# Rings, load distance and MLP order at the end of a four-layer network kernel

## The chip, the cores and the metric

The kernel runs on one core of a Trainium2 chip. The metric is device time in microseconds; the kernel before has a median of 9638.22 us over three runs (9626.88 to 9641.67). Everything is float32.

## The reference

Four layers, each `x + layer(group_norm(x))`, on `x` of 8 x 384 x 32 x 32: (0) a Mamba block, (1) deformable convolutions, (2) a Mamba block with an MLP behind it, (3) a shift layer. The change is at the end of layer 2 and in layer 3.

```python
# layer 2, after the scan
t = y @ out_proj_w.T
t = gelu(t @ mlp_w1.T + mlp_b1) @ mlp_w2.T + mlp_b2        # 384 -> 1536 -> 384
# layer 3: 48 groups of 8 channels, each with its own offset
disp = _displace(x, round(offset))                          # zero outside the image
kernel = exp(-|grid + offset - round(offset)|^2 / 0.5)      # 5 x 5, normalized
out = depthwise_conv(disp, kernel)
```

The 5 x 5 kernel is a product of a column and a row factor, so displacement and convolution together are one 32 x 32 matrix over y and one over x for each group of channels.

## The kernel before, in words

One program does the four layers one after another. Layers 0 and 2 share `ssm_layer`. It goes over 16 steps (8 samples, two halves of TS = 512 tokens), and each step has 48 units (6 blocks of 128 channels, 8 pairs of states) of the scan. PE, ScalarE (ACT), VectorE (DVE) and GpSimd (POOL) get their instructions in an order written out by hand (`plan` and the loop after it). SP, which issues most DMAs, isn't in that list (`ENGINES`), so the framework's scheduler orders SP's queue; an engine's queue is worked off in order.

In layer 2 the output projection and the MLP of a step run beside the next step's scan. For the last step there is no next scan, and they stand after the loop, together with preparations of layer 3:

- `out_proj` (L500) for three blocks of output channels, `out_take` (L517, ACT) copies them to `t`.
- `kernels_a` (L1455 to L1481) and `kernels_b` (L1486 to L1500) make the matrices of the shift layer: small DVE and ACT work, at the end four ACT copies into `sbd` (L1500).
- The MLP goes over three quarters of its 1536 hidden channels, q = 0, 1, 2, each of four blocks of 128 (`NF // 4` is 3). `mlp_up` (L528) makes four products into PSUM (`ps_h`, from a ring of three buffers), `up_take` (L535, ACT) adds the bias and writes them to `hid` (one buffer, pool `p1`), `gelu` (L538, ACT) works on the whole `hid`, `mlp_down` (L545) makes three products from it (`ps_m`, the same PSUM ring), and `down_take` (L552, L554, DVE) adds them to `x`. At q = 2 it also stores the block to the DRAM tensor `x3s` (L506, SP).
- `stat_load` (L1506) and `stat` (L1512, L1514, DVE) gather the group norm's statistics of layer 3 from the 15 earlier half samples; `some(5)` does five of them in each q, and `stat(last, ...)` does the last half sample's as its blocks are finished.
- Weights come by `w_mid` (L246, SP) into the ring `wm` of three buffers.

The shift layer is `shift_parts`. It has 12 tiles m (`NM`) of 4 groups of 8 channels: 128 partitions are 4 groups x 32 rows, the free dimension is 8 channels x 8 samples x 32 columns. A half tile is a piece c (24 in all) of 128 x 1024. For each piece: `scale` (L1592, POOL) multiplies by the norm's factor; `over_y` (L1602, L1604, PE) applies the matrix over y and adds the norm's offset into the PSUM tile `ps_y`; `turn` (L1608, DVE) transposes 32 x 32 blocks into `syt`; `over_x` (L1614, PE) applies the matrix over x; `turn_back` (L1620, DVE) transposes back into `szt`; `add` (L1625, POOL) adds to the tile `sxr`. After the second piece 32 stores go out (L1629), 16 from SP and 16 from ACT's queue, each of 32 partitions and one channel to `out`, in runs of 32 floats. `load` (L1573) brings a tile by four DMAs from SP.

`main` is a software pipeline: in iteration i it emits `scale(i+3)`, `over_y(i+2)`, `over_x(i+1)`, `turn(i+2)`, `turn_back(i+1)`, `add(i)`. The first three tiles are loaded before it, and tile m is loaded three tiles ahead:

```python
for m in range(3):
    load(m)
norms()
main()
```

Buffers come from rings (a pool's tag with a number of buffers) left over from the scan: `bc` with 8 buffers of 8 KB per partition, `hs` with 4 and `db` with 3 of 4 KB, `wm` with 3 of 6 KB. Before, `sxr` and `sxa` (the scaled tile) both come from `bc`, as do the statistics' half samples `sx` and the tables `se`, `skr` and `ssel`; `syt` comes from `hs`, `szt` from `db`. `norms` (L1523 to L1563) finishes the statistics and makes the table `stab` that `scale` and `over_y` read.

Of the kernel before, what the change touches and what calls it, by code (L numbers as in the profile page):

```python
# [8 lines left out]
F32 = mybir.dt.float32  # L9
# [6 lines left out]
P = 128  # L16
C = 384
G = C // P
# [5 lines left out]
NS = 16  # L24
RK = C // 16
RB = RK + 2 * NS
TS = L // 2
W_MID = 1536
# [6 lines left out]
NF = FF // P  # L35
# [49 lines left out]
class Net:  # L85
# [107 lines left out]
    def ssm_layer(self, li, src, dst, shift=None):  # L193
# [3 lines left out]
        with ExitStack() as ctx:  # L197
            wp = ctx.enter_context(tc.tile_pool(name=f"w{li}", bufs=1))
            p1 = ctx.enter_context(tc.tile_pool(name=f"p1_{li}", bufs=1))
            p2 = ctx.enter_context(tc.tile_pool(name=f"p2_{li}", bufs=2))  # L200
# [32 lines left out]
            def v(i):  # L233
                return vec[:, i : i + 1]
# [8 lines left out]
            def w_mid(src, k):  # L243
                t = p2.tile([P, k, W_MID // k], F32, name="wm", tag="wm", bufs=3)
                n = src.shape[2]
                nc.sync.dma_start(out=t[:, :, :n], in_=src)  # L246
                return t
# [97 lines left out]
            def exp_ln():  # L345
                nc.scalar.preload_act_table_set("natural_log_exp_and_others")
# [155 lines left out]
            def store(s, o):  # L502
                if mlp:

                    y = s["h"] * H // 2
                    nc.sync.dma_start(  # L506
                        out=shift[0][o * P : (o + 1) * P, y : y + H // 2, s["b"] * W : (s["b"] + 1) * W],
                        in_=s["x"][:, o, :].rearrange("p (y x) -> p y x", x=W),
                    )
                if o == G - 1 and (not mlp or s is not steps[-1]):  # L510
                    nc.sync.dma_start(out=dst(s["b"])[:, :, s["sl"]], in_=s["x"])
# [11 lines left out]
            def mlp_up(s, q, f):  # L523
                if f == 0:
                    s["w1"] = w_mid(w1_d[:, :, q * 4 * P : (q + 1) * 4 * P], G)
                s["up", f] = ps = self.psum("ps_h")
                for k in range(G):
                    nc.tensor.matmul(  # L528
                        ps, s["w1"][:, k, f * P : (f + 1) * P], s["t"][:, k, :], start=(k == 0), stop=(k == G - 1)
                    )  # L530

            def up_take(s, q, f):
                if f == 0:
                    s["hid"] = p1.tile([P, 4, TS], F32, name="hid")
                nc.scalar.activation(s["hid"][:, f, :], s["up", f], AF.Identity, bias=v(V_B1 + 4 * q + f))  # L535

            def gelu(s):
                nc.scalar.activation(s["hid"], s["hid"], AF.Gelu)  # L538

            def mlp_down(s, q, o):  # L540
                if o == 0:
                    s["w2"] = w_mid(w2_d[:, 4 * q : 4 * q + 4, :], 4)
                s["down", o] = ps = self.psum("ps_m")
                for f in range(4):
                    nc.tensor.matmul(  # L545
                        ps, s["w2"][:, f, o * P : (o + 1) * P], s["hid"][:, f, :], start=(f == 0), stop=(f == 3)
                    )

            def down_take(s, q, o):
                xo = s["x"][:, o, :]  # L550
                if q == 0:
                    nc.vector.scalar_tensor_tensor(xo, s["down", o], v(V_B2 + o), xo, ALU.add, ALU.add)  # L552
                else:
                    nc.vector.tensor_tensor(xo, xo, s["down", o], ALU.add)  # L554
                if q == NF // 4 - 1:
                    store(s, o)

            steps = []
# [88 lines left out]
            with tc.manual_schedule(engines=ENGINES):  # L647
                s = steps[0]
# [29 lines left out]
                for i, (s, j, m) in enumerate(units):  # L678
                    c, t = divmod(i, T)
# [38 lines left out]
                    k = 3 if mine else 2 if m in gp_add else 1  # L718
# [16 lines left out]
                if mlp:  # L735
                    kernels_a()

                    def some(n):
                        for _ in range(min(n, len(stats))):
                            i = stats.pop(0)  # L740
                            for g in range(G):
                                stat(i, loaded["x", i], g)
                            if i + 6 < last:
                                stat_load(i + 6)

                    for q in range(NF // 4):
                        for f in range(4):
                            mlp_up(s, q, f)
                            up_take(s, q, f)
                        gelu(s)  # L750
                        if q == NF // 4 - 1:
                            exp_ln()
                        some(5)
                        if q == 0:
                            kernels_b()
                        for o in range(G):
                            mlp_down(s, q, o)
                            down_take(s, q, o)
                            if q == NF // 4 - 1:
                                stat(last, s["x"], o)  # L760
                    for m in range(3):
                        load(m)
                    norms()
                    main()
# [656 lines left out]
    def shift_parts(self, wp, p2, dap, src_of, srcs, dst):  # L1421
        nc, ins, nb = self.nc, self.ins, self.nb
        NM = NP // IG
        NQ = P // IG
        M2 = 2 * NM
        d = {}

        def ring(tag, shape, name, bufs=None):
            kw = {"bufs": bufs} if bufs else {}
            t = p2.tile(shape, F32, name=name, tag=tag, **kw)  # L1430
            return t

        def bc(name, *shape):
            t = ring("bc", [P, 2, 2, TS], name, NS // 2).rearrange("p a b l -> p (a b l)")
            n = 1
            for k in shape:
                n *= k
            return t[:, :n]
# [126 lines left out]

        NI = CPP * nb
        CH = NI * W // 2

        def load(m):
            xr = d["xr", m] = bc("sxr", NI, W).rearrange("p (i w) -> p i w", w=W)  # L1570
            for n in range(IG):
                c = (m * IG + n) * CPP
                nc.sync.dma_start(  # L1573
                    out=xr[n * H : (n + 1) * H].rearrange("p (k b) w -> p k (b w)", k=CPP),
                    in_=srcs[c : c + CPP].rearrange("k y b -> y k b"),
                )

        def table(c, t):
            m, h = divmod(c, 2)
            g, q = divmod(m, NQ // CPP)  # L1580
            q = q * CPP + h * CPP // 2
            return d["tab"][:, t, g, q : q + CPP // 2].rearrange("p q b -> p (q b)")

        def piece(t, c):
            return t[:, c % 2 * NI // 2 : (c % 2 + 1) * NI // 2].rearrange("p i w -> p (i w)")

        def scale(c):
            m = c // 2
            if c % 2 == 0:
                d["xa", m] = bc("sxa", NI, W).rearrange("p (i w) -> p i w", w=W)  # L1590
            x, xa = (piece(d[k, m], c).rearrange("p (i w) -> p i w", w=W) for k in ("xr", "xa"))
            nc.gpsimd.tensor_tensor(xa, x, table(c, 0).unsqueeze(2).to_broadcast([P, NI // 2, W]), ALU.mult)  # L1592

        def mat(c, t):
# [1 line left out]

        def over_y(c):
            ps = d["psy", c] = dap.tile([P, 2, TS], F32, name="ps_y", tag="da").rearrange("p a b -> p (a b)")[:, :CH]
            xa = piece(d["xa", c // 2], c)
            for i in range(0, CH, HL):  # L1600
                o = ps[:, i : i + HL]
                nc.tensor.matmul(o, mat(c, 1), xa[:, i : i + HL], start=True, stop=False)  # L1602
                t = table(c, 1)[:, i // W : i // W + HL // W].unsqueeze(2).to_broadcast([P, HL // W, W])
                nc.tensor.matmul(o.rearrange("p (i w) -> p i w", w=W), mat(c, 1), t, start=False, stop=True)  # L1604

        def turn(c):
            yt = d["yt", c] = ring("hs", [P, 2, TS], "syt", 4).rearrange("p a b -> p (a b)")
            nc.vector.transpose(yt, d["psy", c])  # L1608

        def over_x(c):  # L1610
            d["psx", c] = []
            for i in range(0, CH, HL):
                ps = self.psum("ps_yx")
# [1 line left out]
                d["psx", c].append(ps)  # L1615

        def turn_back(c):
            zt = d["zt", c] = ring("db", [P, 2, TS], "szt", 3).rearrange("p a b -> p (a b)")
            for i, ps in enumerate(d["psx", c]):
                nc.vector.transpose(zt[:, i * HL : (i + 1) * HL], ps)  # L1620

# [12 lines left out]
        def main():  # L1634
            nch = 2 * NM
            for i in range(-3, nch):
                for k, fn in ((3, scale), (2, over_y), (1, over_x), (2, turn), (1, turn_back), (0, add)):
                    if 0 <= i + k < nch:
                        fn(i + k)
                m = i // 2 + 3  # L1640
                if i % 2 and 3 <= m < NM:
                    load(m)

        return d, load_consts, kernels_a, kernels_b, stat_load, stat, norms, load, main
# [93 lines left out]
```

## Time and profile before

| | |
|---|---|
| median of three runs | 9638.22 us |
| profiled execution | 9640.38 us |
| its span, first to last instruction | 9638.6 us |
| mean granted TensorE clock | 0.948 |
| busy in the span: PE, DVE, ACT, POOL | 89%, 84%, 68%, 60% |
| last unit of the scan ends on PE | about 9329 us |
| last MLP and its output projection on PE | 9329.1 to 9419.9 us |
| last statistics on DVE | 9421.6 us |
| first `scale`, last `add` ends | 9432.5, 9629.4 us |

The profile is of one execution. A matmul line is named as line, operation, output and input; a wait line says which instruction waited for which other, with total us, number and longest. In a line of the timeline the brackets at the end give the engine's idle time before the instruction and what ended it. A "q" behind an engine's name means its DMA-issuing queue. Instructions that only issue a DMA don't count as busy. Ends of matmuls are modelled, so neighbouring groups can overlap by some tenths of a microsecond. From 9318 us on, PE is busy for 245 us of 321, POOL for 103, DVE for 117.

### The profile page before, as it was taken

The numbers are of one execution on the slowest core, as the hardware profiler recorded it, in microseconds if no ns is written. First come the engines' busy times: TensorE is split into PE (matmuls) and PEld (weight loads), VectorE is DVE, ScalarE is ACT, GpSimd is POOL, SyncE is SP. The second block draws the span as 40 slices with busy tenths as digits, with TensorE's granted clock in tenths as the row PEclk, the third lists the DMA queues.
The fourth block names the chain that finished last, engine by engine and source line by source line (L and its number), as shares of the span: only waits on it lengthen the run. The fifth ranks groups of instructions, "written<-read, shape, count | busy, mean of one in ns | idle before, by whom it ended". The sixth has DMA issues, their size and how long they took to land. (4 is left out here: it accounts for less than half of the span.)

```text
span 9638.6 us, 87976 instructions
## 1 busy us (share of the span) xinstructions
PE 8594.0 (89%) x28252; PEld 4554.4 (47%) x28252; DVE 8105.5 (84%) x8807; ACT 6508.4 (68%) x10236; POOL 5755.9 (60%) x3788
## 2 busy tenths in 40 slices
PE   6898888888886899999999997699999999999987
PEld 2333333333332677677677776234343443434333
DVE  6999999999996678778778777799999999999973
ACT  5666666666663677778778777667767777776750
POOL 6888888888895000000000000799999999999964
PEclk8999999999998999999999998799999999999998
DMA  2211211121121333333333333133332333223426
GB/s 71 83 58 46 83 52 52 54 81 52 49 80 45 74 77 83 87 81 83 87 82 83 87 81 85 59 121 99 93 93 89 117 111 96 90 91 101 125 95 108
DMA packets 560755, 792.02 MB, mean 82 GB/s; under 512 B 238019, under 2 KB 391011, under 8 KB 536601
## 3 DMA queue, kind: packets, MB, share of 16 engines
q1 hardware_dynamic: 508056, 779.99, 27.8%
q10 hardware_dynamic: 52224, 6.30, 0.4%
q8 instruction: 225, 3.69, 0.2%
q14 instruction: 250, 2.04, 0.1%
HBM read 716.49 MB, written 69.66 MB: 82 GB/s over the span
## 5 line engine op out<-in xcount | busy, mean ns | idle before, releaser
L426 POOL TENSOR_TENSOR db<-du,bc 128x1024 f32<-128x1024 f32 x1536 | 3608.4, 2354 | 421.0 <-DVE hs L436 229.1
L436 DVE TENSOR_TENSOR_SCAN da<-da,db 128x1024 f32<-128x1024 f32 x1272 | 2912.2, 2289 | 200.8 <-ACT da L421 151.0
L467 PE MATMUL y<-hs,ident 128*128 128x512 f32 x5184 | 2610.3, 639 | 384.8 <-DVE hs L450 242.1
L421 ACT ACTIVATE da<-dt,na 128x512 f32<-128x512 f32 x3072 | 2120.2, 691 | 912.9 <-DVE hs L450 683.4
L394 POOL TENSOR_TENSOR dt<-dt,sp_e 128x512 f32<-128x512 f32 x192 | 244.0, 1271 | 3091.0 <-DVE sp_e L386 3091.0
L467 PEld LDWEIGHTS y<-hs,ident 128*128 128x128 f32 x5184 | 1018.2, 203 | 1872.9 <-issue 1142.6
L1407 PE MATMUL wacc<-fsm,fxk 128*128 128x221 f32 (+34 forms) x10624 | 1636.4, 312 | 73.3 <-DVE fsm L1377 71.4
L450 DVE TENSOR_TENSOR hs<-da,bc 128x1024 f32<-128x1024 f32 x1272 | 1557.6, 1225 | 117.1 <-PE y L467 12.7
L1407 PEld LDWEIGHTS wacc<-fsm,fxk 128*128 128x128 f32 x10624 | 1550.0, 193 | 209.3 <-DVE fsm L1377 132.4
L1377 DVE TENSOR_TENSOR fsm<-fhy,fhx 128x170 f32<-128x170 f32 (+42 forms) x3216 | 1172.2, 427 | 430.5 <-PE wacc L1407 415.2
L1337 ACT ACTIVATE fhy<-fpyx,cell 128x416 f32<-128x416 f32 (+9 forms) x1280 | 645.6, 576 | 398.2 <-DVE fsm L1377 398.2
L1095 PE MATMUL ps_off<-fxn,fow 128*32 128x248 f32 (+18 forms) x2944 | 832.7, 523 | 3.8 <-issue 2.0
L1360 DVE TENSOR_TENSOR fxk<-fxt,fwk 128x1024 f32<-128x1024 f32 (+1 forms) x688 | 785.8, 1178 | 6.4 <-ACT fxt L1153 6.4
L436 DVE TENSOR_TENSOR_SCAN hs<-da,db 128x1024 f32<-128x1024 f32 x264 | 602.3, 2282 | 70.2 <-POOL db L414 28.0
L447 POOL TENSOR_TENSOR hs<-hs,bc 128x1024 f32<-128x1024 f32 x264 | 621.8, 2355 | 37.8 <-ACT st L442 37.5
L454 POOL TENSOR_TENSOR hs<-hs 128x512 f32<-128x512 f32 x480 | 609.0, 1269 | 3.5 <-DVE hs L450 3.5
L545 PE MATMUL ps_m<-hid,wm 128*128 128x512 f32 x1152 | 540.4, 614 | 39.7 <-ACT hid L538 34.8
L528 PE MATMUL ps_h<-t,wm 128*128 128x512 f32 x1152 | 536.0, 603 | 16.4 <-DVE x L552 16.4
L1342 ACT ACTIVATE fhy<-fhy,cols 128x1344 f32<-128x1344 f32 (+10 forms) x368 | 530.7, 1442 | 12.0
L1095 PEld LDWEIGHTS ps_off<-fxn,fow 128*98 128x98 f32 (+2 forms) x2944 | 352.7, 147 | 382.2 <-issue 359.2
L442 ACT COPY st<-da 128x2 f32<-128x2 f32 x624 | 97.8, 157 | 506.0 <-DVE hs L450 504.5
L545 PEld LDWEIGHTS ps_m<-hid,wm 128*128 128x128 f32 x1152 | 222.2, 196 | 343.6 <-issue 263.6
(192 smaller groups left out, 9626.7 us busy)
## 6 DMA issues: line engine op xcount, KB each, us to landing
bc<-bcd SPq DMA_DIRECT2D x256, 1024.0 KB
fpyx<-fposd SPq DMA_DIRECT2D x640, 256.0 KB
wm<-in_w SPq DMA_DIRECT2D x96, 768.0 KB
x<-x SPq DMA_DIRECT2D x71, 768.0 KB
winr<-in_win SPq DMA_DIRECT2D x192, 192.0 KB
x<-in_x SPq DMA_DIRECT2D x40, 768.0 KB
fpyx<-fposd SPq DMA_DIRECT2D x24, 1024.0 KB
wm<-in_wout SPq DMA_DIRECT2D x48, 384.0 KB
```

The costliest lines, as they stand in the source:

```text
L421: nc.scalar.activation(da[:, i, :], s["dt", j], AF.Exp, scale=na[:, j, n : n + 1])
L426: nc.gpsimd.tensor_tensor(db, du, s["bc"][m][:, 0], ALU.mult)
L436: nc.vector.tensor_tensor_scan(h1, da1, db1, 0.0, ALU.mult, ALU.add)
L447: nc.gpsimd.tensor_tensor(s["hs", m], s["hs", m], c, ALU.mult)
L450: nc.vector.tensor_tensor(hs, s["da", m], c, ALU.mult)
L467: nc.tensor.matmul(s["y"], self.ident, s["hs", m][:, i, :], start=first and i == 0, stop=k == NU - 1 and i == n - 1,)
L545: nc.tensor.matmul(ps, s["w2"][:, f, o * P : (o + 1) * P], s["hid"][:, f, :], start=(f == 0), stop=(f == 3))
L1095: nc.tensor.matmul(o[:, ya - r0 : yb - r0, xa:xb], ow[:, (dy + pad) * K + dx + pad, :], x3[:, ya + dy : yb + dy, xa + dx : xb + dx], start ...
L1337: nc.scalar.activation(hy[:, at : at + (yb - ya) * W], pyx[:, 0, ya * W : yb * W], AF.Abs, bias=bias)
L1360: nc.vector.tensor_tensor(t[:, :n], x, wk[:, j : j + 1, :].to_broadcast([P, n, P]), ALU.mult)
L1377: nc.vector.tensor_tensor(self.sub(sm, at, [(r * w, n), (w, r), (1, w)]), self.sub(hy, hy_at[by] + xa, [(r * W, n), (W, r), (1, w)]), self ...
L1407: nc.tensor.matmul(a[:, ya - 4 * o : yb - 4 * o, xa:xb], k, self.sub(sm, sm_at[by], [(w, yb - ya), (1, w)]), start=False, stop=False,)
```

## The change

The rings of layer 3 are given out anew: the scaled pieces `sxa`, now one buffer for each half tile, take `hs`; `syt` takes `db`; `szt` takes `wm`; the loaded tiles `sxr` keep `bc`. Six tiles are loaded before `main`, and each later tile six tiles ahead. In the last step's MLP the first products of a third come ahead of the second products of the third before it (up 0, up 1, down 0, up 2, down 1, down 2), so two `hid` are alive: the one of q = 1 of the last step takes a buffer of `bc`. The statistics are divided 4, 6 and 5 instead of 5, 5 and 5, and from q = 1 on they stand after `down_take` instead of before `mlp_down`.

```diff
             def up_take(s, q, f):
                 if f == 0:
-                    s["hid"] = p1.tile([P, 4, TS], F32, name="hid")
+                    if s is steps[-1] and q == 1:
+                        t = p2.tile([P, 2, 2, TS], F32, name="hid1", tag="bc", bufs=NS // 2)
+                        s["hid"] = t.rearrange("p a b l -> p (a b) l")
+                    else:
+                        s["hid"] = p1.tile([P, 4, TS], F32, name="hid")
+                    s["hid", q] = s["hid"]
...
-                        ps, s["w2"][:, f, o * P : (o + 1) * P], s["hid"][:, f, :], start=(f == 0), stop=(f == 3)
+                        ps, s["w2"][:, f, o * P : (o + 1) * P], s["hid", q][:, f, :], start=(f == 0), stop=(f == 3)
...
-                    for q in range(NF // 4):
-                        for f in range(4):
-                            mlp_up(s, q, f)
-                            up_take(s, q, f)
-                        gelu(s)
-                        if q == NF // 4 - 1:
-                            exp_ln()
-                        some(5)
+                    NQ = NF // 4
+                    for q in range(NQ + 1):
+                        if q < NQ:
+                            for f in range(4):
+                                mlp_up(s, q, f)
+                                up_take(s, q, f)
+                            gelu(s)
+                            if q == NQ - 1:
+                                exp_ln()
                         if q == 0:
+                            some(4)
                             kernels_b()
+                            continue
                         for o in range(G):
-                            mlp_down(s, q, o)
-                            down_take(s, q, o)
-                            if q == NF // 4 - 1:
+                            mlp_down(s, q - 1, o)
+                            down_take(s, q - 1, o)
+                            if q == NQ:
                                 stat(last, s["x"], o)
-                    for m in range(3):
+                        some(6)
+                    for m in range(6):
                         load(m)
...
+        AHEAD = 6
...
         def scale(c):
             m = c // 2
-            if c % 2 == 0:
-                d["xa", m] = bc("sxa", NI, W).rearrange("p (i w) -> p i w", w=W)
-            x, xa = (piece(d[k, m], c).rearrange("p (i w) -> p i w", w=W) for k in ("xr", "xa"))
+            d["xa", c] = ring("hs", [P, 2, TS], "sxa", 4).rearrange("p a b -> p (a b)")
+            x, xa = (t.rearrange("p (i w) -> p i w", w=W) for t in (piece(d["xr", m], c), d["xa", c]))
...
-            xa = piece(d["xa", c // 2], c)
+            xa = d["xa", c]
...
-            yt = d["yt", c] = ring("hs", [P, 2, TS], "syt", 4).rearrange("p a b -> p (a b)")
+            yt = d["yt", c] = ring("db", [P, 2, TS], "syt", 3).rearrange("p a b -> p (a b)")
...
-            zt = d["zt", c] = ring("db", [P, 2, TS], "szt", 3).rearrange("p a b -> p (a b)")
+            zt = ring("wm", [P, G, W_MID // G], "szt", 3).rearrange("p a b -> p (a b)")
+            zt = d["zt", c] = zt[:, :CH]
...
-                m = i // 2 + 3
-                if i % 2 and 3 <= m < NM:
+                m = i // 2 + AHEAD
+                if i % 2 and AHEAD <= m < NM:
                     load(m)
```

## The prediction, made before the result was known

> **What bounds the kernel now.** I read the page's engine slices first: only the last of 40 changes character (POOL's row ends 9, 9, 6, 4 and DMA's rises). The diff touches the end of layer 2 and the shift layer alone: its hid ring edit asks for the last step, and for every other step the new key of `hid` names the same tile. So I read the waits of 9318 to 9640 us, then the timelines of that stretch, then small windows of DMA. The columns of waits are total us, times, longest us.
>
> ```profile
> DVE syt L1608 <- PE ps_y L1604: 136.1, 24, 12.6
> POOL sxa L1592 <- DMA out<-sxr: 74.9, 8, 10.2
> POOL sxa L1592 <- DMA sxr<-x3s: 10.0, 1, 10.0
> PE ps_y L1602 <- POOL sxa L1592: 46.9, 9, 7.0
> PE ps_m L545 <- ACT hid L538: 9.4, 3, 4.0
> ```
>
> POOL's scaling of a new tile waits for DMA 9 times, 84.9 us, PE waits for POOL and DVE for PE: one chain, begun by DMA. SP's own waits:
>
> ```profile
> SPq L1629 <- POOL sxr L1625: 35.8, 13, 10.9
> SPq L1573 <- DMA out<-sxr: 30.9, 12, 4.1
> SPq L1629 <- DMA out<-sxr: 26.5, 28, 1.5
> ```
>
> SP waits for POOL too, so it is a circle. One turn of it, from SP's and POOL's timelines:
>
> ```profile
> 9513.83 12.86 SPq L1629 DMA_DIRECT2D out<-sxr  x16
> 9526.79 4.78 SPq L1573 DMA_DIRECT2D sxr<-x3s  x4
> ```
> ```profile
> 9518.64 1.91 POOL L1592 TENSOR_TENSOR sxa<-sxr,stab 128x1024 f32<-128x1024 f32 x1 [9.83 <-DMA out<-sxr]
> 9536.20 1.91 POOL L1592 TENSOR_TENSOR sxa<-sxr,stab 128x1024 f32<-128x1024 f32 x1 [9.17 <-DMA out<-sxr]
> ```
>
> The scaling at 9518.64 lets `add` run; it ends at 9522.9, the second half of that tile's stores is issued from 9522.9 to 9526.7, the loads of the tile three ahead stand behind them in SP (9526.8 to 9531.6), and when they have landed the scaling at 9536.20 starts. From 9482.10 to 9609.03, seven turns take 18.1 us each. Nothing is full in that time: 4.25 us of POOL a half tile (1.91 + 2.34), 2.5 us of DVE, and 5.15 us of PE (its L1614 groups start at 9441.72, 9446.87, 9452.02 and 9457.17 while input is there), so 10.3 us a tile.
>
> The last MLP before it, on PE:
>
> ```profile
> 9344.54 10.46 PE L528 MATMUL ps_h<-t,wm 128*128 128x512 f32 x24
> 9359.01 12.26 PE L545 MATMUL ps_m<-hid,wm 128*128 128x512 f32 x24 [4.00 <-ACT hid L538]
> 9371.11 10.46 PE L528 MATMUL ps_h<-t,wm 128*128 128x512 f32 x24
> 9384.29 10.57 PE L545 MATMUL ps_m<-hid,wm 128*128 128x512 f32 x24 [2.72 <-ACT hid L538]
> 9394.69 10.46 PE L528 MATMUL ps_h<-t,wm 128*128 128x512 f32 x24
> 9407.88 11.99 PE L545 MATMUL ps_m<-hid,wm 128*128 128x512 f32 x24 [2.72 <-ACT hid L538]
> ```
>
> Each second product waits for the gelu of its own first product: 9.44 us idle, and 1.8 and 1.5 us more where a group runs slow after it.
>
> **What the Trainium skill says.** "TensorE: Matmul & The Clock Gate", Part 1, What's actually happening: after an idle window of about 3.4 us the array runs at half its clock until it has been busy for about as long. The trace agrees: after 5 to 7 us of idle a pair of L1602 takes 2.07 us, and 1.02 in a full stretch. "DMA: Bandwidth & Descriptors", Why small descriptors are slow: there is a fixed cost per packet and per descriptor. The trace agrees: stores go out in 128 B runs and move 121 GB/s, loads in 1 KB runs 199. The columns after the stretch are busy us of PE, PEld, DVE, ACT and POOL with counts, then PE clock, DMA share and GB/s:
>
> ```profile
> 9514.50:9518.50 4.00, 0.41 (x1) 0.00 (x0) 1.18 (x2) 0.00 (x0) 0.00 (x0) 1.00 1.02 199
> ...
> 9628.00:9636.00 8.00, 0.00 (x0) 0.00 (x0) 0.00 (x0) 0.00 (x0) 1.37 (x1) 0.58 0.79 121
> ```
>
> The first row is loads with few stores, the second stores alone. The same page, Rules for kernel authors, says that DMAs of SP and ACT run on the same 16 engines and that spreading them saves only issue time; SP's and ACT's stores beside each other do not go over 121 GB/s here, so I add stores and loads up, not their queues.
>
> **The change part by part.** The profiled run took 9640.38 us and its span 9638.6, so 1.8 lie outside; its run stands 2.2 above the median 9638.22. I sum on the span and carry the difference to the median.
>
> MLP. Removed: the three gelu waits (9.44 us) and the slow starts (3.3), as PE now does up 0, up 1, down 0, up 2, down 1, down 2. Six groups of 10.45 from 9344.5 end at 9407.2, where they end at 9419.9 now. Cover: gelu 0 is done at 9358.95, up 1 runs to 9365.4. Added: `hid1` takes a buffer of the bc ring, so its first write can wait for one; `se` is free after L1495 (9350.2), `skr` after the sbd copies. Those four copies (0.92 each) stand ahead of up_take 1 on ACT and end at 9362.2; behind them PE's fourth group of up 1 needs a PSUM buffer (three in the ring) at 9362.8. I take 0; bounds 0 and 4 us (a whole sbd pass uncovered); no gain is possible from an added wait. w1 of q 1 is wanted 16 us earlier (9355, not 9371); SP issued it at 9344.5 with w2; 768 KB at the 199 GB/s of the loads above are 3.9 us, 7.9 if it shares, so it is in time; bound 0 to 4 us again. up 2 writes `hid` after down 0 has read it: PE's own order covers it.
>
> What comes last is then DVE, not PE. A statistics step costs 2.13 us (10.9 us for five, 9371.98 to 9382.86). `some(6)` stands after down_take 0 (9376.6) and costs 12.8, to 9389.4, as down 1 delivers: covered. The last five stand after down_take 1 (9397.5) and cost 10.2 (as 9395.5 to 9405.7), to 9407.7, and only then come three times 0.69 + 0.69 + 0.21, to 9412.7. Now it is 9421.57. So the MLP is worth **8.9 us**, not 12.7. `some(4)` and kernels_b after the first gelu lie in DVE time that waits for PE. norms and tables follow as now, so the first half tile's store starts at 9446.95 - 8.9 = 9438.1.
>
> Shift layer, six loads ahead. Three more tiles are 12 DMAs of 256 KB, and 24 in all stand in SP ahead of the first stores. They start when the last x3s write is issued (9411.7) and go every 1.3 us when the engines are full (9426.84, 9428.19, 9429.47 now), to 9443: 6 us of them are left at 9438.1. The first tile's four are first in line, so the first scaling isn't late. After that a load of tile m stands behind the stores of tile m - 6, and is used about four tiles of PE time later: at 10.3 us a tile that is 41 us, against 9 to 10 us that POOL waits now. So the 84.9 us of POOL's wait go.
>
> Rings. sxa leaves bc for hs (four half tiles, three ahead plus the one read), so bc's eight hold xr alone: seven tiles are alive between load and store, and one spare covers stores that land. syt moves to db (three; alive for two iterations), szt to wm (three, as it had). No instruction is added; waits for these rings: 0, bound 0 to 0.4 us a half tile (4 against 3 buffers of syt, one of PE's L1614), 0 to 10 us.
>
> What is late next: PE or DMA. **PE**: first product at 9434.85 - 8.9 = 9425.9, 24 half tiles at 5.15 are 123.6, so 9549.5; from PE's last end (9625.5) to the span's end are 13.1 us now: 9562.6. **DMA**: a tile is 1.05 MB, 8.7 us of stores at 121 GB/s and 5.2 us of loads at about 200. From 9438.1: 6 of loads left over, 12 x 8.7 = 104 of stores, 6 x 5.2 = 31 of loads: 141 us, so 9579.6, and 2.4 from the last issue (9636.2 now) to the end: **9582.0**. Stores used only 0.79 of DMA; if loads filled the rest (6.9 us a tile, 82 in all) it would be 9560 and PE would decide. Upward, mixed stretches stall SP; at 15 us for a tile with loads instead of 13.9 it is 9589. I take the sum without overlap, since 9527 to 9530, with both kinds, showed a share of 0.79 as well.
>
> Issue time is no bound: 0.5 us each, 16 + 4 a tile on SP is 10 us, and 16 on ACT is 8.
>
> Sum: 9582.0 - 9638.6 = -56.6, of which 8.9 are the MLP. Median 9638.2 - 56.6 = **9582**.
>
> **The rivals.** (1) Forecast, DMA paces: 9570 to 9605. (2) PE paces, loads slip into the stores' gaps: 9562.6 in span, 9562 median. For it: the share of 0.79; against: SP's 28 waits of stores on stores. (3) POOL's wait is exchanged for SP's own: stores keep 12.8 us and loads 4.8 a tile as in the timeline, now not as an echo of POOL. Six tiles at 17.6 and six at 12.8 are 182, so 9438.1 + 182 + 2.4 = 9623, median 9622. For it: 57.4 us of SP's waits are for DMA. Against: in the drain, 32 stores take 9.1 us. (4) Slower: each of a tile's four loads waits for a store of the tile whose buffer it takes, in SP, with the next tile's stores queued behind it. At the longest such wait, 4.1 us, that is 16.4 + 12.9 of stores, 29.3 us for the six tiles with loads: 6 x 29.3 + 6 x 12.9 = 253, so 9438 + 253 + 2.4 = 9693, median 9693. It makes the kernel slower from 20.2 us a tile on (six of them with six at 12.9 reach 9638.6). Against: the buffer is that of a tile stored a tile or two before.
>
> **How the numbers follow.** (1) 0.60, (2) 0.20, (3) 0.14, (4) 0.06. The predicted time is that of (1). About 0.2% (19 us) is what can be told from no change, so faster is below 9619. (1), (2) and a third of (3) are faster: 0.85; the rest of (3) is the same: 0.09; (4) slower: 0.06. The range takes (2) with 4 us below and (1) with the 4 us bounds of the MLP and the rings' 10: 9558 to 9613.
>
> **What would show it.** Right: no wait of sxa on DMA to speak of; PE's shift groups 5.15 us apart to about 9550; the last adds by 9555, and then a tail of stores alone of 15 to 25 us; DMA share near 0.8 from 9440; ps_m without a wait on hid; the last statistics at 9412 to 9413, behind other statistics on DVE. Wrong: PE gaps of 5 us or more between tiles (3 or 4), the tail shorter than 12 us (2), or a wait for w1 or hid1 at 9355 to 9363.

## The result and the profile after

| | before | after |
|---|---|---|
| median | 9637.44 us (4 runs) | 9606.45 us (4 runs, 9605.35 to 9607.43) |
| ratio, 95% interval | | 0.9969 [0.9952, 0.9987] |
| profiled execution, its span | 9640.38, 9638.6 us | 9605.35, 9603.5 us |
| MLP: start of the last `out_proj` to first `ps_y` | 105.8 us | 98.0 us |
| shift layer: first `ps_y` to the span's end | 203.7 us | 180.6 us |
| `scale` waits for a load | 9 times, 84.9 us | 3 times, 26.6 us |

The median fell by 31.0 us, and the two stretches give the same sum: 7.8 + 23.1 = 30.9. The prediction had 8.9 + 47.7 = 56.6; the 24.6 us that are missing from the shift layer (47.7 - 23.1) are the question. So the MLP did nearly what was forecast, and the shift layer half of it. Where `out_proj` starts differs by up to 12 us between profiles, with every layer ahead of it unchanged. So from here on stretches are compared, and medians, but not single spans.

The MLP on PE, from the timeline after:

```profile
9340.39 18.19 PE L528 MATMUL ps_h<-t,wm 128*128 128x512 f32 x42
9358.73 2.84 PE L528 MATMUL ps_h<-t,wm 128*128 128x512 f32 x6 [0.15 <-ACT hid L540]
9361.41 10.46 PE L550 MATMUL ps_m<-hid,wm 128*128 128x512 f32 x24
9371.71 10.46 PE L528 MATMUL ps_h<-t,wm 128*128 128x512 f32 x24
9382.01 20.76 PE L550 MATMUL ps_m<-hid,wm 128*128 128x512 f32 x48
```

Six groups follow each other without a gap but one of 0.15 us; the three waits for gelu (9.44 us) are gone.

The waits that answer to those of before (total us, times, longest us), first those of the engines, then those of SP's own queue:

```profile
DVE syt L1618 <- PE ps_y L1614: 89.7, 24, 13.4
...
POOL sxa L1602 <- DMA out<-sxr: 26.6, 3, 10.2
...
PE ps_y L1612 <- POOL sxa L1602: 14.8, 3, 8.1
```
```profile
SPq L1584 <- DMA out<-sxr: 32.0, 13, 6.7
...
SPq L1640 <- DMA out<-sxr: 22.0, 20, 5.4
SPq L1584 <- DMA sxr<-x3s: 17.7, 17, 2.3
...
SPq L1640 <- DMA sxr<-x3s: 8.3, 2, 6.2
```

Nine waits of POOL are three now, each about as long as before. SP's wait for POOL (35.8 us before) is down to 0.3 us, but its loads (L1584) wait for *stores* as long as before, 32.0 against 30.9 us, and the longest such wait has grown from 4.1 to 6.7 us. One turn of what is left, from SP's and POOL's timelines:

```profile
9511.00 8.57 SPq L1640 DMA_DIRECT2D out<-sxr  x16
9519.61 8.52 SPq L1584 DMA_DIRECT2D sxr<-x3s  x4
9528.23 9.52 SPq L1640 DMA_DIRECT2D out<-sxr  x16
9537.80 8.19 SPq L1584 DMA_DIRECT2D sxr<-x3s  x4
9546.09 55.09 SPq L1640 DMA_DIRECT2D out<-sxr  x96
```
```profile
9514.33 1.91 POOL L1602 TENSOR_TENSOR sxa<-sxr,stab 128x1024 f32<-128x1024 f32 x1 [6.92 <-DMA out<-sxr]
...
9532.96 1.91 POOL L1602 TENSOR_TENSOR sxa<-sxr,stab 128x1024 f32<-128x1024 f32 x1 [10.23 <-DMA out<-sxr]
...
9550.80 1.91 POOL L1602 TENSOR_TENSOR sxa<-sxr,stab 128x1024 f32<-128x1024 f32 x1 [9.46 <-DMA out<-sxr]
```

Four loads, 2 us of issuing, keep SP for 8.5 us, where they kept it for 4.8 before. POOL waits for just those loads: tiles 9, 10 and 11, the last ones. After 9546 only stores are left in SP, and it works on them until 9601.2. ACT's queue, which has half the stores and no load, is done much earlier:

```profile
9437.32 139.15 ACTq L1640 DMA_DIRECT2D out<-sxr  x192
```

It ends at 9576.5, 24.7 us ahead of SP. Nor were the DMA engines full. The columns are us, busy us of PE, PEld, DVE, ACT and POOL with counts, PE clock, DMA share and GB/s; first the stretch with loads, then the tail, then the part of the tail in which ACT is done:

```profile
9438.00:9546.00 108.00, 98.10 (x224) 42.87 (x223) 43.99 (x54) 0.00 (x0) 73.89 (x35) 0.95 0.74 133
9546.00:9601.00 55.00, 16.14 (x33) 6.58 (x31) 8.77 (x11) 0.00 (x0) 15.38 (x7) 0.66 0.59 95
9576.00:9601.00 25.00, 0.00 (x0) 0.00 (x0) 0.00 (x0) 0.00 (x0) 0.00 (x0) 0.50 0.44 68
```

Stores alone had a share of 0.79 and 121 GB/s before, with two queues issuing. In the tail they now have 0.59 and 95 on average, and only 0.44 and 68 in its last 25 us, when SP alone issues them, one in about 0.49 us.

### The profile page after: what moved, and what is told of

It is laid out like the page before. It is cut to its first block, busy times and chain, and to the rows that moved or that the text cites. A ratio compares the mean times of both kernels' runs of the same rounds, so it can differ in the third digit from the quotient of the medians.

```text
span 9603.5 us, 87989 instructions
## 1 busy us (share of the span) xinstructions
PE 8576.2 (89%) x28252; PEld 4549.0 (47%) x28252; DVE 8106.0 (84%) x8807; ACT 6509.3 (68%) x10236; POOL 5760.4 (60%) x3788
## 5 line engine op out<-in xcount | busy, mean ns | idle before, releaser
L1334 ACT ACTIVATE fhx<-fpyx,cell 128x544 f32<-128x544 f32 (+8 forms) x640 | 380.1, 666 | 0.0
```

## The experiments

**Two theories.** C: the DMA engines, or six tiles of distance as such, set the pace, so that the 24.6 us are bytes that the sum had too cheap. A: the *order of issue* sets it. In the built program each DMA of SP or ACT signals one of eight completion semaphores (counters that a queue can wait for), and these are dealt out in turn over both queues, in the order in which the framework's scheduler laid the DMAs out. A DMA waits first for the one before it on its semaphore, also where the other queue issued that one. The Trainium skill, "DMA: Bandwidth & Descriptors", Why a DMA increments its semaphore by 16 and not by 1, gives a reason for such a wait: with two DMAs in flight on one semaphore a wait can be over before the first has landed. No run here shows that case, only the wait.

SP has 20 DMAs for a tile (16 stores, 4 loads), ACT 16. In the laid-out order the stores of the two queues mostly alternate, but up to four of ACT's stores follow each load of SP, so in a tile with loads ACT gains up to 16 stores, a whole tile, on SP. (Why the framework lays it out so stays open.) Tile 6's loads stand behind ACT's stores of tile 1 at the latest, tile 8's behind those of tiles 4 and 5: the lag builds up. A stretch after the change, read from the program's waits and not from the profile (S or A for the queue, L for a load, s for a store, then the tile):

```
... SL9 As6 As6 As6 As6 SL9 As7 As7 As7 As7 SL9 As7 As7 As7 As7 SL9 Ss4 ...
... SL10 As8 As8 As8 As8 SL10 SL10 SL10 Ss5 ...
... SL11 As9 As9 As9 As9 SL11 SL11 SL11 Ss6 ...
```

In SP the load of tile 10 stands ahead of the stores of tile 5; in the common order it stands behind ACT's stores of tile 8, two tiles before its own, and those wait for tile 8's `add`. The trace's single issues fit: the first load of tile 10 is issued at 9519.61 and the second at 9526.82, 1.7 us after the store of tile 8 that it has to wait for (ACT, 9525.12); tile 11's at 9537.80 and 9544.68, 1.7 us after tile 9's (9542.98). The wait is not for the buffer: with eight buffers the load of tile 10 takes that of tile 2, whose stores were issued by 9484.3, 35 us earlier. So, by A, six tiles ahead in the code are two ahead in effect for the last tiles, and the gain in this layer came from the three more tiles already there at its start and the lead that they give the next loads.

**1. The MLP's part alone**: the kernel before with the loop of the last MLP, `hid1` and the statistics as changed, rings and loads as they were.

> The kernel before with the MLP order (and hid1, and the statistics 4, 6, 5) alone; rings and load distance of before. The two profiles give the MLP 7.8 us up to PE's first product of the shift layer. Theory (the parts add up): 9630 median, the shift layer's 203.7 us from first product to the end unchanged. Rival (the earlier start is lost again, since the first loads set the pace): 9637, and the first scaling waits for a load.

Measured 9626.87 us (12 runs, 9619.83 to 9633.14), ratio 0.9992 [0.9983, 1.0000]; before beside it 9637.35. The interval reaches 1.0000, so the medians alone don't show this part; the stretch does. The MLP's stretch is 98.0 us, as in the whole change and in the profiles of experiments 3, 4, 8 and 9; the shift layer takes 204.1 us, with nine waits as before.

**2. The shift layer's part alone**: the changed kernel with the MLP loop of before.

> The changed kernel with the last MLP in its old order; rings and six tiles ahead stay. Theory: the shift layer takes 180 us from first product to the end instead of 203.7, so 9614 median, with three waits of POOL for a load, at tiles 9, 10 and 11. Rival (the 24 loads get in the way of the stores only because the MLP ends earlier): over 9625.

Measured 9611.87 us (15 runs), ratio 0.9974 [0.9966, 0.9982]. MLP 105.8 us, shift layer 182.5, three waits of 27.4 us in all. By stretches the two parts add up, 7.8 us and 21.2 against 7.8 and 23.1 in the whole. By medians they gave 10.5 and 25.5 us, 36 against 31.0, which their intervals allow. No loss between the two parts is seen.

**3. New rings, old distance.**

```diff
-        AHEAD = 6
+        AHEAD = 3
...
-                    for m in range(6):
+                    for m in range(3):
                         load(m)
```

> The changed kernel with three tiles ahead instead of six; new rings and MLP order stay. Theory A (what the shift layer gains is three tiles more in store at its start; after that a load of tile m waits in SP for stores of tile m - 2 from ACT's queue, whatever the distance in the code): POOL waits for a load about 8 times again, the shift layer takes about 203 us, 9629 median. Theory B (it was the ring shared by loaded and scaled tiles that made loads late): gain kept, about 9606 to 9612.

Measured 9629.85 us (12 runs), ratio 0.9994 [0.9985, 1.0003]; MLP 98.0, shift layer 202.0 us. The waits:

```profile
POOL sxa L1602 <- DMA out<-sxr: 83.5, 9, 10.7
```

Nine waits, as before. The rings do nothing by themselves; what helped is the loads. The edit takes back both the three tiles more at the start and the distance, so it doesn't tell these two apart.

**4. Later loads from GpSimd's queue**, which has neither SP's order nor its semaphores.

```diff
-                nc.sync.dma_start(
+                (nc.gpsimd if m >= AHEAD else nc.sync).dma_start(
                     out=xr[n * H : (n + 1) * H].rearrange("p (k b) w -> p k (b w)", k=CPP),
```

> The changed kernel with the loads of tiles 6 to 11 issued from POOL's queue instead of SP's, so that they share neither a queue nor a semaphore slot with the stores. Theory A (loads are late because SP's load waits for ACT's stores of two tiles before): no wait of POOL for a load, PE's pieces 5.15 us apart to the end, stores limited by DMA, 9575 to 9588, less what issuing costs POOL. Theory C (16 DMA engines are full in the stretches with loads and stores, 17.3 us a tile): the six tiles with loads keep 17 us, 9603 to 9610.

Measured 9571.6 us (4 runs, 9567.05 to 9577.75), ratio 0.9933 [0.9916, 0.9949]; shift layer 147.4 us. No scaling waits for a load. The stores, from the timelines of SP and of ACT:

```profile
9441.51 131.73 SPq L1640 DMA_DIRECT2D out<-sxr  x192
```
```profile
9440.96 132.42 ACTq L1640 DMA_DIRECT2D out<-sxr  x192
```

Both queues end together. The same bytes, loaded at the same distance in the code, took 33 us less, so C falls. This run alone can't say whether SP's order of instructions or the shared semaphores did it, since GpSimd's queue is free of both.

**5 to 7. Fewer stores in SP**, so that SP lags ACT less, by A: 14, 12 and 10 of a tile's 32 stores from SP (16 in the changed kernel), all else alike. The edit for 12:

```diff
-                        (nc.sync if n % 2 else nc.scalar).dma_start(
+                        (nc.sync if n == 3 or (n == 1 and k % 2 == 0) else nc.scalar).dma_start(
```

For 14 the condition is `n % 2 and (n, k % 4) != (1, 0)`, for 10 it is `n == 3 or (n == 1 and k % 4 == 0)`.

> The changed kernel with 14 of a tile's stores in SP and 18 in ACT's queue (16 and 16 before); the loads stay in SP behind the stores of the tile six before. In the program's waits the loads of tiles 9, 10 and 11 then share their semaphore slots with ACT's stores of tiles 5 and 6, 7, and 8 and 9 instead of 6 and 7, 8, and 9. Theory A (that is the wait): waits of POOL for a load get fewer or shorter, 9590 to 9602. Rival (a load in SP simply comes too late behind SP's stores): as many waits as before less the 1 us of issue time per tile, 9603 to 9607.

> As the kernel with 14, but 12 stores of a tile in SP and 20 in ACT's queue; the loads of tiles 9, 10 and 11 share slots with ACT's stores of tiles 4 and 5, 6, and 7 and 8, about four tiles before. Theory A: at most one short wait of POOL for a load, 9578 to 9592. Rival: still three waits, 9600 to 9607.

> As the kernel with 14, but 10 stores of a tile in SP and 22 in ACT's queue; the loads of tiles 9, 10 and 11 share slots with ACT's stores of tiles 3 and 4, 5, and 6. Theory A: no wait of POOL for a load, PE's pieces 5.15 us apart to the end; ACT's queue issues 264 stores, 132 us at 0.5 us each, so 9572 to 9590. Rival (loads in SP are late anyway, or 16 DMA engines are full): 9595 to 9610.

| stores of a tile from SP | tiles of the ACT stores that the loads of tiles 9; 10; 11 stand behind | waits of `scale` | last issue after first `ps_y`: SP, ACT | shift layer | median, ratio |
|---|---|---|---|---|---|
| 16 (the change) | 6 to 7; 8; 9 | 3, 26.6 us | 177.8, 153.1 | 180.6 us | 9606.45, 0.9969 |
| 14 | 5; 7; 8 to 9 | 2, 12.3 us | 159.3, 142.8 | 162.1 us | 9587.57, 0.9948 [0.9931, 0.9964] |
| 12 | 4; 5 to 6; 7 | 1, 4.6 us | 146.2, 148.6 | 151.5 us | 9574.63, 0.9936 [0.9920, 0.9953] |
| 10 | 3 to 4; 4 to 5; 6 | 0 | 133.3, 160.0 | 162.8 us | 9588.41, 0.9951 [0.9934, 0.9967] |

This is a graded answer, and no count of bytes changes in it: each step takes away waits as the laid-out order says, until with 10 the longer queue, ACT's 22 stores a tile, sets the end instead. With 14 and 12 the times came out some 3 us below their ranges. The number of DMAs alone doesn't explain it: with 14 each queue has 18 for a tile with loads, and SP still ends 16.5 us after ACT; with 12, SP has 16 and ACT 20, and they end together.

**8. Seven tiles ahead** (`AHEAD = 7` and `range(7)`), stores as in the change.

> The changed kernel with seven tiles loaded first and seven ahead instead of six. Theory A (only the tiles in store at the start help; each one more saves one wait of some 8 us): two waits of POOL for a load, at tiles 10 and 11, and 9596 to 9600. Rival C (the sum of DMA time sets the end): the same bytes in the same stretch, 9604 to 9608.

Measured 9593.2 us, ratio 0.9957 [0.9940, 0.9973]; shift layer 170.3 us. One wait was left (5.6 us, tile 11), not two, and the time was 3 to 7 us better than expected: one more tile in store saved two waits. In this kernel's laid-out order tile 10's loads stand behind ACT's stores of tiles 6 and 7, tile 11's behind those of tiles 8 and 9. SP's last issue is at 167.5, ACT's at 134.7.

**9. Loads halved between the queues**: of the four loads of a late tile, two from ACT and two from SP. Stores, semaphores and both queues stay; each queue now has 18 DMAs for such a tile, as with 14 stores from SP, but also the same two loads. In the laid-out order a late load now stands behind stores of tile m - 6, and the queues keep step.

```diff
-                nc.sync.dma_start(
+                (nc.scalar if m >= AHEAD and n % 2 == 0 else nc.sync).dma_start(
                     out=xr[n * H : (n + 1) * H].rearrange("p (k b) w -> p k (b w)", k=CPP),
```

> Of the six later loads, two of a tile's four DMAs go from ACT's queue and two from SP's, so each queue has 18 DMAs for such a tile; stores are as in the changed kernel. Theory A (SP with 20 falls behind ACT with 16, and a load waits for ACT's stores of the tile two before it): in the program's order load 9 now stands behind stores of tile 3 and load 11 behind tile 5, so no wait of the scaling on a load, both queues' last stores within 3 us of each other, and 9568 to 9582 us. Rival C (the DMA engines, or six tiles of distance as such, pace it): the same loads and the same distance in the code give 9600 to 9608 and three waits.

Measured 9575.08 us (4 runs, 9569.68 to 9578.81), ratio 0.9934 [0.9917, 0.9950]; shift layer 149.3 us, no wait of the scaling on a load. SP's timeline, and then one window over all stores:

```profile
9501.72 1.69 SPq L1584 DMA_DIRECT2D sxr<-x3s  x2
9504.95 9.38 SPq L1640 DMA_DIRECT2D out<-sxr  x16
9514.38 1.62 SPq L1584 DMA_DIRECT2D sxr<-x3s  x2
9517.09 52.33 SPq L1640 DMA_DIRECT2D out<-sxr  x96
```
```profile
9440.00:9571.00 131.00, 109.11 (x255) 48.01 (x253) 52.79 (x66) 0.00 (x0) 89.34 (x42) 0.93 0.87 149
```

Two loads keep SP for 1.6 us, not 8.5 for four. The DMA share is 0.87 with 149 GB/s for the whole stretch. SP ends 2.5 us ahead of ACT. This is the narrowest of the tests: twelve DMAs of 256 KB change their queue, and 31 us go.

**10. The mirror**: all late loads from ACT's queue (`nc.scalar if m >= AHEAD else nc.sync`), so that ACT has 20 DMAs for a tile and SP 16.

> The mirror of the changed kernel: the six later loads go from ACT's queue, so ACT has 20 DMAs for such a tile and SP 16. Theory A: ACT now falls behind, load 10 stands behind SP's stores of tile 8 and load 11 behind those of tile 9; two or three waits of the scaling (12 to 30 us), SP's last store 15 to 27 us ahead of ACT's, 9598 to 9608. Rival (it is SP itself that is slow, or loads have to leave SP): no wait, 9570 to 9585.

Measured 9607.64 us (5 runs, 8 of before), ratio 0.9964 [0.9950, 0.9978]; shift layer 184.1 us.

```profile
POOL sxa L1602 <- DMA out<-sxr: 29.3, 3, 10.9
```
```profile
9522.33 9.70 ACTq L1584 DMA_DIRECT2D sxr<-x3s  x4
9532.12 9.62 ACTq L1640 DMA_DIRECT2D out<-sxr  x16
9541.78 8.21 ACTq L1584 DMA_DIRECT2D sxr<-x3s  x4
9550.08 56.02 ACTq L1640 DMA_DIRECT2D out<-sxr  x96
```

The picture of the changed kernel with the queues' names exchanged, 8 to 10 us for four loads now in ACT; SP's last store is 25 us ahead of ACT's. So it is not SP that is slow: with stores shared evenly, the queue that has all the loads falls behind.

No run changes the semaphores and leaves the order alone. That the wait is theirs rests on the program's waits, the two issue times that fit them, and the table of experiments 5 to 7.

**11. Twelve stores from SP and seven tiles ahead.**

> 12 of a tile's stores from SP and 20 from ACT, and seven tiles loaded ahead. Theory A: the one wait left with twelve (4.6 us) goes, but the first store comes 4 to 5 us later, behind four more loads, and what ends last is the sum of bytes: 9570 to 9580, no better than with six ahead (9574.6). Rival: distance still pays, 9560 to 9569.

Measured 9579.55 us, ratio 0.9940 [0.9924, 0.9957]; shift layer 157.1 us, no wait. Four more loads ahead of the first stores and no wait left to save: not better than six ahead.

The best versions are 4, 5 to 7 with twelve, and 9, at 9571.6, 9574.6 and 9575.1 us; their runs overlap, so none of the three is shown to be the best. All three are some 31 to 35 us below the changed kernel.

## Why the prediction was half right

- **The number**: inside the stated range, by luck. 9606 is 24 us above the 9582 named, and just outside the 9570 to 9605 of the forecast itself. What was to widen the range upward, the bounds of `hid1`, w1 and the rings (4, 4 and 10 us), takes 9582 to 9600 and not to 9613, and none of these waits came. Of its signs, POOL's waits for loads (6.9 to 10.2 us) and PE's gaps at tiles 9, 10 and 11 (1.8, 8.1 and 4.9 us) point to what it had named for rivals (3) and (4).
- **What bound the kernel**: right. POOL waiting for a load, PE for POOL, SP for stores; each wait that an experiment took away brought the end nearer.
- **MLP, 8.9 us**: right in kind, 1.1 too much. The last statistics came 9.5 us earlier (92.5 to 83.0 us after the start of `out_proj`; 9407.95 in the trace, behind other statistics on DVE as said, and 4 us earlier than the 9412 to 9413 named, mostly since `out_proj` started 4 us earlier). "norms and tables follow as now" gave back 1.7 us, most of it in one place: the fourteen small products of L1533 took 3.17 us, and 1.74 before. PE now ends its MLP 5 us ahead of the statistics instead of running up to them. `hid1` and w1 waited for nothing that shows.
- **Rings, 0 of 0 to 10 us**: right (experiment 3).
- **PE and the tail**: not reached by the change. With the loads halved, the last `add` ends 128.0 us after the first product and 21.3 us of stores follow, within the 15 to 25 named; in the changed kernel it ends at 148.0 and 32.6 follow.
- **The step that failed** is "After that a load of tile m stands behind the stores of tile m - 6 ... So the 84.9 us of POOL's wait go", and with it the 13.9 us for a tile with loads. It holds for SP's own stores. By the completion semaphores a load also stood behind ACT's stores of tile m - 2, and 26.6 us of the wait stayed. Term by term: SP's six tiles with loads took 9442.5 to 9546.1, 17.3 us each and not 13.9, which is 20.2 us in all; its six without took 55.1, 9.2 each and not 8.7, which is 2.9; and its first store came 19.6 us after the first `ps_y`, where the sum had 12.2 and 6 of loads (9443 less 9438.1 is 4.9), which is 1.4. Together 24.5, of the 24.6 that were missing.
- **The DMA sum itself** was nearly right as a price for the engines. Experiment 9 did what the sum describes: SP's tiles with loads took 12.1 us each (9444.3 to 9517.1), those without 8.7, from first to last store 132.7 us in place of 141. Its 9575 us stand 7 below the forecast of 9582: loads and stores overlapped a little, where the sum had no overlap.
- **The rivals.** (3), SP's own waits in place of POOL's, named the size for tiles with loads, 17.6 us, and missed the tail, for which it took 12.8 us a tile and which took 9.2. (4), loads in SP that wait for stores with the next stores behind them, is the form in which it came: one to four waits a tile (6.7 us at most, not four of 4.1), and for a semaphore rather than a buffer. Had one asked which DMA ends SP's 30.9 us of loads waiting for stores *before*, since no buffer called for it (each late load took the buffer of a scaled tile, last read by PE), the two queues' order would have come up. The prediction took that wait for part of the circle that the longer distance would break.

## What to carry to other kernels

Before giving loads more distance, ask what a load waits for where it is issued, besides its buffer: a wait of the DMA queue on transfers of another tile means that the issue order, not the distance in the code, sets how far ahead it is. Where two queues share completion semaphores, read the order in which their DMAs were laid out, and see how far the other queue has got where a load stands. An equal number of DMAs in each is not enough (14 stores from SP: 18 and 18, two waits left). Two things worked here: the same share of loads and of stores in each queue, or fewer stores in the queue that has the loads. A queue that ends long before the other in the timelines, 25 us in the changed kernel, is a reason to look.

## What the runs showed of the hardware

- Where DMAs are issued was worth 31 us at the same bytes. The Trainium skill, "DMA: Bandwidth & Descriptors", Issuing engines are not separate DMA queues, says that issuing from several engines saves only the time it takes to issue. Issue time shows in the changed kernel's last 25 us, where SP alone, at 0.49 us a store, moved 68 GB/s and two queues had moved 121. But twelve loads that left SP saved far more than the 6 us of their issuing (12 at 0.5 us), because waits stood in the queue with them.
- A share of 0.79, which the prediction had taken for full in mixed stretches as well, was no ceiling: stores and loads together reached 0.87 and 149 GB/s over 131 us.
- Less work just ahead of a chain of small products made that chain slower. It is L1523 before and L1533 after. The timeline before, then windows before and after, which have PE's clock ahead of DMA share and GB/s:

```profile
9421.62 1.74 PE L1523 MATMUL gn_ps<-smv,gmat 128*128 128x16 f32 x14 [1.40 <-DVE smv L1514]
```
```profile
9422.00:9424.00 2.00, 1.36 (x13) 1.26 (x12) 0.54 (x3) 0.00 (x0) 0.00 (x0) 1.00 0.89 176
```
```profile
9408.00:9412.00 4.00, 3.17 (x14) 3.06 (x14) 0.69 (x4) 0.00 (x0) 0.00 (x0) 0.50 0.97 186
```

The clock is 1.00 before and 0.50 after, when PE had been busy for only 0.9 us since 9402.8. It agrees with the Trainium skill, "TensorE: Matmul & The Clock Gate", Part 1, What's actually happening, which gives half rate after an idle window of about 3.4 us. It cost 1.4 us of the MLP's gain.
